# Slot masks stored by the sort and read back in the attention sums, edge masks scaled on ScalarE, and smaller first score batches

## The chip, the core and the metric

The kernel runs on one core of a Trainium2 chip. The metric is the device time of one execution in microseconds (us). A core has five engines that work side by side, each through its own queue in order: TensorE (PE, with its weight loads listed as PEld), VectorE (DVE), ScalarE (ACT), GpSimd (POOL) and SyncE (SP), which issues most DMA transfers. Engines wait for each other by semaphores.

## What is computed

A graph with 6250 nodes and 100000 edges, sorted by target node `dst`, and 128 features. Two graph layers, each followed by a residual and a layer norm:

```python
# layer 0, twice: h = x @ W
norm = dinv[src] * ew * dinv[dst]
out = segment_sum(h[src] * norm[:, None], dst) + b
# layer 1
z = h @ fc_w.T;  rh = r_h @ fc_r_w.T           # r_h: one row per edge
e = z[src] @ aw[0] + z[dst] @ aw[1] + rh @ aw[2]
e = where(e >= 0, e, 0.01 * e)
ex = exp(e - segment_max(e, dst)[dst])
alpha = ex / segment_sum(ex, dst)[dst]
agg = segment_sum(alpha[:, None] * (z[src] + rh), dst)
out = relu(agg + z @ loop_w)
```

## The kernel before, in words

**Chunks and slots.** The edges are cut into NC = 49 chunks of CC = 2048 (16 to a partition). In each chunk `sort` gives every edge a slot: a partition 0 to 127 (`pm`) and one of G = 17 groups (`pg`), so that an edge lies on one of the 32 slots that its source node's block of 128 nodes has in a group (the overflow goes to the last five groups). Twelve of the groups are served from a table of node rows in SBUF (`hot`), by matmuls with a 0/1 mask (line 475); the other five, `far`, by indirect DMA (line 484). `sort` works in batches of seven chunks. Its second half (lines 749 to 764) makes for each chunk two masks on VectorE, `ohm` (128 x 2048 bf16: which partition) and `ohg` (128 x 272 bf16: which group), multiplies `ohg` with the edge's record into `put`, and moves the records to their slots with 16 matmuls (line 763). `pm` and `pg` of all chunks stay in SBUF.

**Stages.** Preparation and degrees (to about 150 us), the first node table, then three passes over the 49 chunks:
- First convolution, 245 to 730 us. The sort's steps are dealt out between its chunks. `slot_rows` (line 833) reads each chunk's row of source numbers, spread to all partitions; `slot_masks` compares it (line 837) and stores the mask for later (line 838). Both transfers, and the sort's own store (line 773), go through SP's queue.
- Second table, and second convolution, 790 to 1224 us, in an order written out by hand. It reads the masks back (line 975), and also multiplies the edge features with a row (line 964).
- Attention. `scores` is a generator of steps: `ends` and `starts` gather the two node terms of each edge (`starts` takes a chunk in two halves: line 1071 makes a mask of a row `rk` read from DRAM, 48 matmuls of line 1078, then `sel` and `asr` on VectorE, lines 1081 and 1082); `softmax` (line 1086) works on one batch of chunks as a chain of scans, small matmuls and transfers. `batches` (line 69) sets the batch sizes: 2, 5, then 7. The sums of a batch can begin when its softmax is done.
- Sums (line 1238 on), one chunk after the other, with the next batch's score steps dealt between. `shares` (line 1180) makes `ohm` and `ohg` again from `pm` and `pg`, multiplies `ohg` with the attention shares `al3`, and moves them to the slots: `swt`, the scale of the gathered rows. `pick` gathers the rows and scales them (ScalarE, line 480), `weigh` scales five narrow masks (ScalarE, line 514), `scatter` adds rows into a window of 144 target nodes (TensorE, line 521), one chunk late. `edge_part` (line 1195) does the edge features: `ms` (128 x 16 x 32) says which of 32 targets an edge belongs to, and is multiplied by the share (line 1211, VectorE); 32 matmuls (line 1222) take it with the features `et`; ScalarE copies the result (line 1227); four more matmuls place it.

**Order.** Except in the second convolution, the order on each engine comes from a planner at build time. It takes the instructions by their place in the program, and lets a later one go first where an earlier one, by its own estimate, can't start yet. Buffers are rings: a tile with `bufs=1` is written again only when its readers are done.

Of the kernel before, what the change touches and what calls it, by code (L numbers as in the profile page):

```python
# [10 lines left out]
BF16 = mybir.dt.bfloat16  # L11
I32 = mybir.dt.int32
AF = mybir.ActivationFunctionType
OP = mybir.AluOpType
# [5 lines left out]
P = 128  # L20
# [5 lines left out]
TC = 16  # L26
CC = P * TC
NL = CC // P
WC = 144
WS = 32  # L30
# [8 lines left out]
def gnn_kernel(ctx, tc, x, src, dst, ea, ew, W1, b1, W2, b2, fcw, fcrw, attn, loopw, out):  # L39
# [11 lines left out]
    nc = tc.nc  # L51
# [14 lines left out]
    NC = CF + 1  # L66
    assert 9 <= NC <= 64

    batches, c0 = [], 0
    while c0 < NC:  # L70
        n = min((2, 5)[len(batches)] if len(batches) < 2 else 7, NC - c0)
        batches.append((c0, n))
        c0 += n
    NT = len(batches)
# [3 lines left out]
    G = GP + GS  # L78
# [17 lines left out]
    dram = ctx.enter_context(tc.tile_pool(name="dram", bufs=1, space=DRAM))  # L96
    keep = ctx.enter_context(tc.tile_pool(name="keep", bufs=1))
# [5 lines left out]
    asd_d = dram.tile([NB * P, 2], F32, name="asd_d")  # L103
    md = dram.tile([NB * P, 1], F32, name="md")
    masks = dram.tile([NC, P, GP * P], BF16, name="masks")

    adgd = dram.tile([(NC * NL + 2) * P], F32, name="adgd")
    shd = dram.tile([NC * CC], F32, name="shd")
# [16 lines left out]
    iotab = const.tile([P, WJ], BF16, name="iotab")  # L125
# [11 lines left out]
    iota_t = const.tile([P, P, TC], BF16, name="iota_t")  # L137
# [47 lines left out]
    sdst = keep.tile([P, NC, G], BF16, name="sdst")  # L185
    swt = keep.tile([P, NC, G], F32, name="swt")
    sidx = keep.tile([P, NC, GS], I32, name="sidx")

    pm = keep.tile([P, NC, TC], BF16, name="pm")
    pg = keep.tile([P, NC, TC], BF16, name="pg")  # L190

    dlb = keep.tile([P, NC, TC], BF16, name="dlb")
    rels = keep.tile([P, NC, NL], BF16, name="rels")
# [233 lines left out]
    def out_of(sum_x, sum_r, b0, n, xp, pool, tag):  # L427

        some = blocks[b0 : b0 + n]
        fin = xp.tile([P, 4, D], F32, name="fin", bufs=1)  # L430
        load_some(nc.sync, fin, x1d, b0, n)
        yield
        agg = pool.tile([P, 4, D], F32, name="agg", tag=tag)
        for b, nb in some:
            of = slice(b * P, b * P + nb)
            nc.tensor.matmul(agg[:nb, b - b0, :], sum_r[:, of], wfrT, start=True, stop=False)
            nc.tensor.matmul(agg[:nb, b - b0, :], sum_x[:, of], ident, start=False, stop=True)
        for p, k in whole(some, b0):
            nc.vector.scalar_tensor_tensor(fin[:p, k, :], agg[:p, k, :], 0.0, fin[:p, k, :], op0=OP.max, op1=OP.add)
        yield  # L440
        yield from normed(fin, some, b0, xp)
        store_blocks(nc.sync, out, fin, b0, n)
# [93 lines left out]
    grp = ed.tile([P, NC, TC], BF16, name="grp")  # L536
# [132 lines left out]
    BATCH = 7  # L669
    spilled = keep.tile([P, NC], F32, name="spilled")  # L670
    sorting = ctx.enter_context(ExitStack())
    sp = sorting.enter_context(tc.tile_pool(name="sort", bufs=2))
# [3 lines left out]
    nc.vector.memset(go_on, 1.0)  # L676
    nc.vector.memset(go_on[:, :, 0:1], 0.0)

    def sort():

        for c0 in range(0, NC, BATCH):
# [4 lines left out]
            for c in cs:  # L686
# [24 lines left out]
                k = BP  # L711
# [29 lines left out]

            nc.vector.tensor_tensor(t_, m_i[:, :n, :], r_, op=OP.subtract)
            nc.vector.tensor_mul(t_, t_, o)
            nc.vector.tensor_add(pm[:, some, :], r_, t_)
            nc.vector.scalar_tensor_tensor(t_, k_i[:, :n, :], float(GP), grp[:, some, :], op0=OP.add, op1=OP.subtract)
            nc.vector.tensor_mul(t_, t_, o)
            nc.vector.tensor_add(pg[:, some, :], grp[:, some, :], t_)
            slots = sp.tile([P, BATCH, NF], F32, name="slots")
            for c in cs:
                ohm = sp.tile([P, P, TC], BF16, name="ohm")  # L750
                nc.vector.tensor_tensor(ohm, iota_t, pm[:, c, None, :].to_broadcast([P, P, TC]), op=OP.is_equal)  # L751
                ohg = sp.tile([P, TC, G], BF16, name="ohg")
                nc.vector.tensor_tensor(ohg, iotab[:, None, :G].to_broadcast([P, TC, G]),
                                        pg[:, c, :, None].to_broadcast([P, TC, G]), op=OP.is_equal)
                put = sp.tile([P, TC, NF], BF16, name="put")
                nc.vector.tensor_tensor(put[:, :, : G * F].rearrange("p t (g f) -> p t g f", f=F),  # L756
                                        ohg[:, :, :, None].to_broadcast([P, TC, G, F]),
                                        rec[:, c, :, None, :].to_broadcast([P, TC, G, F]), op=OP.mult)
                nc.vector.tensor_tensor(put[:, :, G * F :], ohg[:, :, GP:],  # L759
                                        blk[:, c, :, None].to_broadcast([P, TC, GS]), op=OP.mult)  # L760
                ps = ps_c.tile([P, NF], F32, name="rec")
                for t in range(TC):
                    nc.tensor.matmul(ps, ohm[:, :, t], put[:, t, :], start=t == 0, stop=t == TC - 1)  # L763
                nc.scalar.copy(slots[:, c - c0, :], ps)
                yield
# [247 lines left out]
    with tc.tile_pool(name="look", bufs=2) as lp, tc.tile_pool(name="conv3", bufs=2) as wp, \  # L1013
# [162 lines left out]
        def deal(count):  # L1176
            for _ in range(count):
                next(steps, None)

        def shares(c, al3, i):  # L1180

            ohm = mp.tile([P, P, TC], BF16, name="ohm", bufs=1)
            nc.vector.tensor_tensor(ohm, iota_t, pm[:, c, None, :].to_broadcast([P, P, TC]), op=OP.is_equal)
            ohg = mp.tile([P, TC, G], BF16, name="ohg", bufs=1)
            nc.vector.tensor_tensor(ohg, iotab[:, None, :G].to_broadcast([P, TC, G]),
                                    pg[:, c, :, None].to_broadcast([P, TC, G]), op=OP.is_equal)
            put = mp.tile([P, TC, G, 3], BF16, name="put", bufs=1)
            nc.vector.tensor_tensor(put, ohg[:, :, :, None].to_broadcast([P, TC, G, 3]),
                                    al3[:, i, :, None, :].to_broadcast([P, TC, G, 3]), op=OP.mult)
            ps = ps_c.tile([P, G, 3], F32, name="rec")  # L1190
            for t in range(TC):
                nc.tensor.matmul(ps, ohm[:, :, t], put[:, t], start=t == 0, stop=t == TC - 1)  # L1192
            nc.vector.tensor_reduce(swt[:, c, :], ps, AX.X, OP.add)

        def edge_part(c, aw, i):

            k = min(NL, -(-(E - c * CC) // P))
            full = k if c < CF else crem // P
            ets = []
            for s0 in range(0, k, NL // 2):  # L1200
                et = mp.tile([P, NL // 2, D], F32, name="et", bufs=3)
                e0, m = c * CC + s0 * P, min(max(full - s0, 0), NL // 2)
                if m:
                    nc.sync.dma_start(et[:, :m, :], ea[e0 : e0 + m * P, :].rearrange("(s p) f -> p s f", p=P))
                if s0 <= full < min(k, s0 + NL // 2):
                    nc.sync.dma_start(et[: crem % P, m, :], ea[e0 + m * P : E, :])
                ets.append(et)
            ms = mp.tile([P, NL, WS], F32, name="ms", bufs=1)
            nc.vector.tensor_tensor(ms, iota[:, None, :WS].to_broadcast([P, NL, WS]),
                                    rels[:, c, :, None].to_broadcast([P, NL, WS]), op=OP.is_equal)  # L1210
            nc.vector.tensor_mul(ms, ms, aw[:, i, :, None].to_broadcast([P, NL, WS]))
            pl = mp.tile([P, NL // 8, WC], F32, name="pl", bufs=1)
            nc.vector.tensor_tensor(pl, iota[:, None, :WC].to_broadcast([P, NL // 8, WC]),
                                    place[:, :, c : c + 1].to_broadcast([P, NL // 8, WC]), op=OP.is_equal)
            ps = ps_r.tile([P, NL // 8, D], F32, name="r")
            for g in range(NL // 8):
                for half in range(2):
                    for q in range(4):
                        s = 8 * g + 2 * q + half
                        if s < k:  # L1220
                            p = P if s < full else crem % P
                            nc.tensor.matmul(ps[WS * q : WS * q + WS, g, :], ms[:p, s, :], ets[g][:p, s % 8, :], start=half == 0,
                                             stop=half == 1 or s + 1 == k)
            sw = mp.tile([P, NL // 8, D], F32, name="sw")
            ng, rest = divmod((k + 1) // 2, 4)
            if ng:
                nc.scalar.copy(sw[:, :ng, :], ps[:, :ng, :])
            if rest:
                nc.scalar.copy(sw[: WS * rest, ng, :], ps[: WS * rest, ng, :])
            ps = ps_c.tile([P, WC], F32, name="rec")  # L1230
            sizes = [P] * ng + ([WS * rest] if rest else [])
            for g, p in enumerate(sizes):
                nc.tensor.matmul(ps, sw[:p, g, :], pl[:p, g, :], start=g == 0, stop=g == len(sizes) - 1)
            return ps

        pieces = Pieces(lambda b0, n: out_of(acc2, sum_r, b0, n, xp, ps_c, "rec"))
        held = None
        for b, (c0, n) in enumerate(batches):
            while b not in ready:
# [212 lines left out]
```

## Time and profile before

| What | us |
|---|---|
| Median of 3 runs (2057.70, 2063.59, 2058.34) | 2058.34 |
| The profiled execution | 2054.54 |
| Its span | 2052.7 |
| Busy in the span: TensorE / VectorE | 1612.4 / 1641.2 |
| Busy in the span: ScalarE / GpSimd | 940.8 / 1097.1 |

The page of the profile shows one execution. Its groups of instructions have the form "line, engine, operation, out<-in, shape, count | busy us, mean ns of one | idle time of the engine just before", and its views of waits name who waited for whom. Over the whole span TensorE and VectorE look alike (79% and 80% busy), so the stages have to be looked at one by one. The mean granted TensorE clock is 0.885. The core moves 306.80 MB by DMA in the span, 149 GB/s.

### The profile page before, as it was taken

The page shows a single profiled execution, that of the slowest core. Times are in us where ns is not written, and L with a number is a line of the kernel's source. Part 1 is how long each engine was busy: PE and PEld are TensorE (multiplying, and loading weights), DVE is VectorE, ACT ScalarE, POOL GpSimd, SP SyncE. Part 2 cuts the span into 40 slices and gives each one's busy share as a digit, 9 for nine tenths or more (in the row PEclk, how much of TensorE's full clock was granted, in tenths as well). Part 3 has the DMA queues.
Part 4 walks back from the last instruction along what each step waited for, and adds up shares of the span by engine and source line. Part 5 has one row for each costly group of instructions (what it writes and reads, how often), then busy time and mean ns, then how long its engine had stood idle before and what let it go on. Part 6 is the DMA issues. An engine that isn't in the chain of part 4 may idle for free.

```text
span 2052.7 us, 78879 instructions
## 1 busy us (share of the span) xinstructions
PE 1612.4 (79%) x33861; PEld 1460.6 (71%) x33861; DVE 1641.2 (80%) x3271; ACT 940.8 (46%) x3096; POOL 1097.1 (53%) x954
## 2 busy tenths in 40 slices
PE   2668689889798886788898885367888888989985
PEld 2456478778788765687787874257777777888885
DVE  8665988779788535899899894589989998998673
ACT  1104355454454655466676773113343434445543
POOL 5001666676675635888788881312434343535662
PEclk9767699899899977899999996568999999999998
DMA  3001343343442625687777775945656666665662
GB/s 70 24 1 37 94 127 112 101 129 95 117 115 70 209 56 193 177 246 222 239 243 244 246 235 156 134 128 139 185 163 192 171 198 171 177 178 158 182 178 67
DMA packets 260707, 306.80 MB, mean 149 GB/s; under 512 B 44121, under 2 KB 199372, under 8 KB 253299
## 3 DMA queue, kind: packets, MB, share of 16 engines
q1 hardware_dynamic: 228741, 244.80, 38.8%
q0 software_dynamic: 23520, 48.22, 11.4%
q10 hardware_dynamic: 8088, 8.65, 1.4%
q8 instruction: 268, 4.39, 0.9%
q14 instruction: 90, 0.74, 0.1%
HBM read 260.35 MB, written 41.23 MB: 147 GB/s over the span
## 4 chain that ended last, share of the span: by engine, by line
DVE 37%; PE 36%; DMA 12%; issue 8%; ACT 5%; POOL 2%; SPq 1%; DVEq 1%; POOLq 0%; ACTq 0%
PE win L521 15%; DVE wm L490 6%; PE g L475 6%; DVE sel L1081 3%; DVE put L756 2%; DMA et<-in_edge_attr_dram 2%; DMA rk<-srow 2%; DMA far<-g,sidx 2%; DMA mask<-srd 2%; DVE et L964 2%; PE rec L1192 2%; ACT got L480 2%; PE mm L332 2%; DVE ohm L751 1%; PE r L706 1%
## 5 line engine op out<-in xcount | busy, mean ns | idle before, releaser
L484 POOL DMA_INDIRECT far<-g,sidx x490 | 707.1, 1443 | 238.6 <-PE win L521 112.0
L480 ACT ACTIVATE got<-g,swt 128x128 f32<-128x128 f32 x1764 | 487.4, 380 | 350.6 <-PE g L475 152.4
L484 POOL DMA_INDIRECT far<-zd,sidx x245 | 311.4, 1271 | 449.9 <-PE win L521 329.1
L521 PE MATMUL win<-wm,got 128*128 128x144 f32 x3528 | 522.0, 306 | 12.4 <-issue 12.2
L521 PEld LDWEIGHTS win<-wm,got 128*128 128x128 f32 x3528 | 485.6, 204 | 30.6 <-issue 21.0
L475 PE MATMUL g<-hot,mask 128*32 128x128 bf16 x21168 | 384.2, 226 | 90.8 <-issue 68.4
L475 PEld LDWEIGHTS <-mask 128*32 128x32 bf16 x21168 | 327.1, 100 | 124.5 <-issue 99.9
L490 DVE TENSOR_TENSOR wm<-iota,sdst 128x1728 f32<-128x1728 f32 x147 | 286.7, 1950 | 4.4 <-DMA g<-rows 4.4
L514 ACT ACTIVATE wm<-wm,swt 128x64 f32<-128x64 f32 (+1 forms) x735 | 203.1, 357 | 99.6 <-DVE wm L497 63.4
L521 PE MATMUL win<-wm,far 128*128 128x64 f32 (+1 forms) x1470 | 186.9, 273 | 11.6 <-DMA far<-g,sidx 11.2
L521 PEld LDWEIGHTS win<-wm,far 128*128 128x128 f32 x1470 | 182.4, 195 | 12.7 <-issue 12.7
L321 POOL TENSOR_TENSOR hot<-low,hot 128x512 bf16<-128x512 f32 x24 | 42.2, 1759 | 199.7 <-DVE own L714 130.4
L1078 PE MATMUL k<-adp,rk 128*128 128x49 bf16 x2352 | 91.4, 194 | 66.3 <-DVE sel L1081 52.0
L1078 PEld LDWEIGHTS <-rk 128*128 128x128 bf16 x2352 | 83.7, 103 | 77.9 <-DVE rk L1071 42.6
L964 DVE TENSOR_TENSOR et<-et,ar_row 128x2048 f32<-128x2048 f32 (+1 forms) x49 | 111.6, 2278 | 23.7 <-DMA et<-in_edge_attr_dram 23.7
L526 DVE TENSOR_TENSOR acc<-acc,win 128x144 f32 x147 | 44.4, 302 | 96.8 <-PE win L521 85.7
L965 DVE TENSOR_REDUCE dots<-et 128x16 f32<-128x2048 f32 (+1 forms) x49 | 112.0, 2286 | 1.7
L763 PE MATMUL rec<-put,ohm 128*128 128x90 bf16 x784 | 62.0, 254 | 34.5 <-DVE put L759 33.6
L763 PEld LDWEIGHTS <-ohm 128*128 128x128 bf16 x784 | 56.9, 165 | 41.4 <-DVE put L759 33.7
L1081 DVE TENSOR_TENSOR sel<-k,ohb 128x392 f32<-128x392 f32 x98 | 83.6, 853 | 2.5 <-PE k L1078 2.1
L756 DVE TENSOR_TENSOR put<-ohg,rec 128x1360 bf16<-128x1360 bf16 x49 | 76.8, 1567 | 0.0
L709 ACT CAST own<-r 128x768 bf16<-128x768 f32 x49 | 39.7, 810 | 75.0 <-PE r L706 49.3
(390 smaller groups left out, 2375.7 us busy)
## 6 DMA issues: line engine op xcount, KB each, us to landing
et<-in_edge_attr_dram SPq DMA_DIRECT2D x97, 512.0 KB
et<-in_edge_attr_dram SPq DMA_DIRECT2D x48, 1024.0 KB
mask<-masks SPq DMA_DIRECT2D x98, 384.0 KB
rk<-srow SPq DMA_DIRECT2D x98, 256.0 KB
mask<-srd SPq DMA_DIRECT2D x49, 384.0 KB
masks<-mask SPq DMA_DIRECT2D x49, 384.0 KB
far<-g,sidx POOLq DMA_INDIRECT x490
g<-rows SPq DMA_DIRECT2D x24, 256.0 KB
```

What stands on the lines that cost most here:

```text
L475: nc.tensor.matmul(ps[32 * q : 32 * q + 32, g, :], mask[:, (g0 + g) * P + 32 * q : (g0 + g) * P + 32 * q + 32], hot[:, 4 * (g0 + g) + q, k ...
L480: nc.scalar.activation(got[:, g, :], ps[:, g, :], AF.Copy, scale=swt[:, c, g0 + g : g0 + g + 1])
L484: nc.gpsimd.indirect_dma_start(out=got, out_offset=None, in_=table[:, :], in_offset=bass.IndirectOffsetOnAxis(ap=sidx[:, c, g : g + 1], ax ...
L490: nc.vector.tensor_tensor(wm[:, : GP * WC].rearrange("p (g w) -> p g w", w=WC), iota[:, None, 1 : WC + 1].to_broadcast([P, GP, WC]), sdst[ ...
L514: nc.scalar.activation(m, m, AF.Copy, scale=swt[:, c, g : g + 1])
L521: nc.tensor.matmul(ps[:, n0 : n0 + m.shape[-1]], rows[g], m, start=g == 0, stop=g == G - 1)
L756: nc.vector.tensor_tensor(put[:, :, : G * F].rearrange("p t (g f) -> p t g f", f=F), ohg[:, :, :, None].to_broadcast([P, TC, G, F]), rec[: ...
L763: nc.tensor.matmul(ps, ohm[:, :, t], put[:, t, :], start=t == 0, stop=t == TC - 1)
L964: nc.vector.tensor_mul(et[:n], et[:n], ar_row[:n, None, :].to_broadcast([n, TC, D]))
L965: nc.vector.tensor_reduce(dots[:n, c, :], et[:n], AX.X, OP.add)
L1078: nc.tensor.matmul(ps[:, s, :], mk[:, s * P : (s + 1) * P], adp[:, 0, k, :NB], start=k == 0, stop=k == 2)
L1081: nc.vector.tensor_mul(sel, ps, ohb.rearrange("p b s -> p s b"))
```

## The change

Three edits go together. The sort now keeps each chunk's two masks in one tile `slot` (128 x 2320 bf16: `ohm` and `ohg` side by side) and stores it to a DRAM tensor `slotd`; `pm` and `pg` become temporaries. The sums read `slotd` back, one chunk ahead, with two buffers. In `edge_part` the product of `ms` and the share becomes up to sixteen activations on ScalarE, one for each run of 128 edges, with the share as the scale. And the batches become 2, 3, 4, 5, then 7 chunks: nine batches instead of eight.

```diff
-        n = min((2, 5)[len(batches)] if len(batches) < 2 else 7, NC - c0)
+        n = min((2, 3, 4, 5)[len(batches)] if len(batches) < 4 else 7, NC - c0)
...
+    slotd = dram.tile([NC, P, P * TC + TC * G], BF16, name="slotd")
...
-    pm = keep.tile([P, NC, TC], BF16, name="pm")
-    pg = keep.tile([P, NC, TC], BF16, name="pg")
...
+    def slot_views(slot):
+        return (slot[:, : P * TC].rearrange("p (q t) -> p q t", t=TC),
+                slot[:, P * TC :].rearrange("p (t g) -> p t g", g=G))
...
-            nc.vector.tensor_add(pm[:, some, :], r_, t_)
+            pm = sp.tile([P, BATCH, TC], BF16, name="pm")
+            pg = sp.tile([P, BATCH, TC], BF16, name="pg")
+            nc.vector.tensor_add(pm[:, :n, :], r_, t_)
...
-                ohm = sp.tile([P, P, TC], BF16, name="ohm")
-                nc.vector.tensor_tensor(ohm, iota_t, pm[:, c, None, :].to_broadcast([P, P, TC]), op=OP.is_equal)
-                ohg = sp.tile([P, TC, G], BF16, name="ohg")
+                slot = sp.tile([P, P * TC + TC * G], BF16, name="slot")
+                ohm, ohg = slot_views(slot)
+                nc.vector.tensor_tensor(ohm, iota_t, pm[:, c - c0, None, :].to_broadcast([P, P, TC]), op=OP.is_equal)
                 nc.vector.tensor_tensor(ohg, iotab[:, None, :G].to_broadcast([P, TC, G]),
-                                        pg[:, c, :, None].to_broadcast([P, TC, G]), op=OP.is_equal)
+                                        pg[:, c - c0, :, None].to_broadcast([P, TC, G]), op=OP.is_equal)
+                nc.sync.dma_start(slotd[c], slot)
...
+        slots_in = {}
+
+        def load_slots(c):
+            if c < NC:
+                slots_in[c] = mp.tile([P, P * TC + TC * G], BF16, name="slot", bufs=2)
+                nc.sync.dma_start(slots_in[c], slotd[c])
+
         def shares(c, al3, i):
-            ohm = mp.tile([P, P, TC], BF16, name="ohm", bufs=1)
-            nc.vector.tensor_tensor(ohm, iota_t, pm[:, c, None, :].to_broadcast([P, P, TC]), op=OP.is_equal)
-            ohg = mp.tile([P, TC, G], BF16, name="ohg", bufs=1)
-            nc.vector.tensor_tensor(ohg, iotab[:, None, :G].to_broadcast([P, TC, G]),
-                                    pg[:, c, :, None].to_broadcast([P, TC, G]), op=OP.is_equal)
+            ohm, ohg = slot_views(slots_in.pop(c))
+            load_slots(c + 1)
...
-            nc.vector.tensor_mul(ms, ms, aw[:, i, :, None].to_broadcast([P, NL, WS]))
+            for s in range(k):
+                nc.scalar.activation(ms[:, s, :], ms[:, s, :], AF.Copy, scale=aw[:, i, s : s + 1])
...
         pieces = Pieces(lambda b0, n: out_of(acc2, sum_r, b0, n, xp, ps_c, "rec"))
+        load_slots(0)
```

More of the change, by code (lines that the diff above doesn't have):

```diff
@@ L743, in sort @@
             nc.vector.tensor_mul(t_, t_, o)
-            nc.vector.tensor_add(pm[:, some, :], r_, t_)
+            pm = sp.tile([P, BATCH, TC], BF16, name="pm")
+            pg = sp.tile([P, BATCH, TC], BF16, name="pg")
+            nc.vector.tensor_add(pm[:, :n, :], r_, t_)
             nc.vector.scalar_tensor_tensor(t_, k_i[:, :n, :], float(GP), grp[:, some, :], op0=OP.add, op1=OP.subtract)
             nc.vector.tensor_mul(t_, t_, o)
-            nc.vector.tensor_add(pg[:, some, :], grp[:, some, :], t_)
+            nc.vector.tensor_add(pg[:, :n, :], grp[:, some, :], t_)
             slots = sp.tile([P, BATCH, NF], F32, name="slots")
             for c in cs:
-                ohm = sp.tile([P, P, TC], BF16, name="ohm")
-                nc.vector.tensor_tensor(ohm, iota_t, pm[:, c, None, :].to_broadcast([P, P, TC]), op=OP.is_equal)
-                ohg = sp.tile([P, TC, G], BF16, name="ohg")
+                slot = sp.tile([P, P * TC + TC * G], BF16, name="slot")
+                ohm, ohg = slot_views(slot)
+                nc.vector.tensor_tensor(ohm, iota_t, pm[:, c - c0, None, :].to_broadcast([P, P, TC]), op=OP.is_equal)
                 nc.vector.tensor_tensor(ohg, iotab[:, None, :G].to_broadcast([P, TC, G]),
-                                        pg[:, c, :, None].to_broadcast([P, TC, G]), op=OP.is_equal)
+                                        pg[:, c - c0, :, None].to_broadcast([P, TC, G]), op=OP.is_equal)
+                nc.sync.dma_start(slotd[c], slot)
                 put = sp.tile([P, TC, NF], BF16, name="put")
```

## The prediction

> **What bounds the kernel now.** I read first the busy times by stretch, with the borders set at the stages (first convolution 245 to 730 us, second 790 to 1224, sums from 1357, the point 1881 where the scores are done). Columns: busy of PE, PEld, DVE, ACT, POOL, granted clock, DMA share, GB/s.
>
> ```profile
> 245.00:730.00 485.00, 421.84 (x9609) 390.68 (x9602) 382.91 (x785) 260.68 (x910) 331.55 (x240) 0.93 0.41 120
> 790.00:1224.00 434.00, 361.02 (x8670) 333.85 (x8674) 394.32 (x422) 285.68 (x937) 356.18 (x235) 0.94 0.75 235
> 1290.00:1357.00 67.00, 25.91 (x495) 22.85 (x497) 46.20 (x117) 4.55 (x13) 15.90 (x12) 0.52 0.86 138
> 1357.00:1406.00 49.00, 31.15 (x647) 27.87 (x639) 42.04 (x131) 10.06 (x38) 6.29 (x5) 0.69 0.51 134
> 1406.00:1881.00 475.00, 407.77 (x9599) 375.55 (x9598) 444.76 (x1055) 188.80 (x646) 203.42 (x165) 0.97 0.63 174
> 1881.00:2033.00 152.00, 138.23 (x3214) 132.22 (x3213) 102.57 (x197) 78.27 (x283) 91.26 (x64) 0.99 0.60 162
> ```
>
> From 1406 to 1881, 33 chunks of the sums run beside the scores: VectorE is 94% busy and TensorE 86%, at 14.4 us a chunk. In the last 14 chunks no scores are left: VectorE falls to 67%, TensorE rises to 91%, 10.9 us a chunk. So the sums are VectorE's first and TensorE's later. The first convolution leaves VectorE a fifth of its time and the DMA engines more than half.
>
> Second, who waits for whom from 1406 to 1881 (us in total, times, longest):
>
> ```profile
> ACT got L480 <- DVE swt L1193: 125.5, 29, 8.5
> ...
> PE rec L1192 <- DVE put L1188: 15.6, 17, 1.6
> PE k L1078 <- DVE sel L1081: 15.4, 17, 3.3
> ...
> DVE rk L1071 <- DMA rk<-srow: 5.6, 4, 3.6
> ```
>
> Both other engines wait for VectorE. ScalarE idles 125.5 us for shares that VectorE delivers late; VectorE itself hardly waits for a transfer.
>
> Third, what the edit touches, as the groups of that stretch and the one line of ohg have it:
>
> ```profile
> L1183 DVE TENSOR_TENSOR ohm<-iota_t,pm 128x2048 bf16<-128x2048 bf16 x33 | 40.1, 1215 | 0.0
> ...
> L1211 DVE TENSOR_TENSOR ms<-ms,aw 128x512 f32<-128x512 f32 x32 | 21.6, 675 | 0.0
> ```
> ```profile
> L1185 DVE TENSOR_TENSOR ohg<-iotab,pg x49: 407/433/472, 1293.4 to 1999.8; 128x272 bf16<-128x272 bf16 x49
> ```
>
> None of the three is preceded by idle time: they are queued back to back, so their removal shortens the queue.
>
> **What the Trainium skill says.** "ScalarE: Activation LUTs", What ACT_TABLE_LOAD costs: an activation takes 186 ns plus 0.833 ns an element, some 93 ns more for each pointer operand, and neighbours overlap by some 93 ns. For 32 columns with a pointer scale an estimate of 306 ns, 213 ns start to start. The trace agrees for the next sizes (ScalarE's timeline, five of 64 columns, then eight of 128):
>
> ```profile
> 1579.50 1.30 ACT L514 ACTIVATE wm<-wm,swt 128x64 f32<-128x64 f32 x5 [1.88 <-DVE wm L497]
> 1582.31 2.18 ACT L480 ACTIVATE got<-g,swt 128x128 f32<-128x128 f32 x8 [1.50 <-PE win L521]
> ```
>
> With one at 0.36 and 0.38 us, (1.30 - 0.36) / 4 is 0.24 us a step at 64 columns, (2.18 - 0.38) / 7 is 0.26 at 128. "TensorE: Matmul & The Clock Gate", Architectural detail, says that ScalarE and VectorE are strictly first in, first out: a waiting instruction holds all behind it. The 125.5 us above are such a wait. "DMA: Bandwidth & Descriptors", Queues, rings and completion order: transfers issued by one sequencer share one ring on each DMA engine, taken in order. So a new store can delay a read issued after it; the trace of before has no such pair to show it.
>
> **The change, part by part.** Each number is against the profiled execution: 2054.5 us for a span of 2052.7; the median of the runs shown is 2058.3, so 3.8 us are added at the end.
>
> *Masks read back.* Per chunk of the sums VectorE loses ohm 1.215 and ohg 0.433. *Edge masks on ScalarE* takes the product ms, 0.68. Together 2.33 us a chunk, for the 35 chunks before 1881: 82 us. *More batches*: nine softmax passes for eight. One costs VectorE 8.6 us (the groups of lines 1102 to 1144 and the splits of al, over six passes, 51.7 us), and ScalarE two table loads of 1.28. The number of end and start steps is the same, their place is not: before chunk 2 can start, three chunks' scores are needed and not five. That is four halves fewer ahead of it, each sel 0.86, asr 0.56, rk 0.48 and ohb 0.35 on VectorE, 9 us; they come back later. The wider row tables (nine rows for eight) add under 1 us in the second convolution, beside its transfers.
>
> So for 1357 to 1881 VectorE has 42.0 + 444.8 - 82 + 8.6 = 413 us of work, TensorE 31.2 + 407.8 + 1.5 for the extra pass = 440. TensorE becomes the longer. How near to 100% it gets is my choice: I take 91%, what it shows in the last 14 chunks where VectorE no longer holds it. 440 / 0.91 = 484 against 524: **-40 us**. Bounds: at the 86% of now 513, -11; at 95%, 463, -61.
>
> *ScalarE's new link.* Sixteen activations at 0.21 to 0.24 us, 3.4 to 3.8 us a chunk (782 in all). From 1406 to 1881 ScalarE is 40% busy and has the room. In the last 14 chunks 5.6 us of 10.9 become 9.1, 84%. There the product lies between the mask on VectorE and TensorE's 32 r matmuls, with 12 got and 5 wm activations in the same queue. The r matmuls start 5 to 9 us after VectorE's product today (1944.0 to 1949.0, 1952.9 to 1960.1), so 3.5 us fit unless the got block goes first. Behind a late r on TensorE stand the rec, next share and next g matmuls. VectorE's saving there is worth nothing. **+4 us**; bounds -2 and +20 (1.4 us a chunk).
>
> *Sort's stores.* 49 of 128 x 2320 bf16, 594 KB each. At the second convolution's rate (235 GB/s at 0.75 share, 313 GB/s full) one holds the engines 1.9 us. VectorE's next use of a slot buffer now waits for its store, two chunks back; behind it stands all of VectorE's work, and TensorE waits for that. On SP the store waits for ohg; behind it stand the masks' stores, the srd store and the srd reads. Those reads already come late in the first convolution (engines' waits there):
>
> ```profile
> DVE mask L837 <- DMA mask<-srd: 29.5, 15, 3.0
> ```
>
> If all 15 grow by 1.9 us, 28 us; if the stores fit between, nothing. Below nothing I exclude, as no work leaves the stage. I take a third: **+9 us**.
>
> *Slot reads.* 49 of 594 KB on SP, a chunk ahead, two buffers. DMA work per chunk of the sums: 0.63 x 14.4 = 9.1 us, plus 1.9 is 11.0 in some 13.3: 83%, more than the 75% of the second convolution. I cost that inside the 91%. Ahead of the sums it is different: between 1290 and 1357 the DMA share is 0.86 and the first rk reads stand on the chain of waits:
>
> ```profile
> 1305.62 11.21 DMA rk<-srow
> ...
> 1322.21 5.79 DMA rk<-srow
> ```
>
> Two slots at that stretch's 138 GB/s are 8.6 us if put ahead of rk, 0 behind: **+4 us**.
>
> Sum: -40 + 4 + 9 + 4 = -23. 2054.5 - 23 = 2031.5 profiled, **2035** as a median.
>
> **The rivals.**
> *TensorE fully fed.* The scores' matmuls (line 1078) fill its gaps, since VectorE then has 15% to spare: 463 us, -61, with +3 elsewhere: 2000. For it: every large wait of TensorE names VectorE. Against it: at 83% DMA share reads arrive later.
> *The gain goes into transfers.* The rk reads run only two halves ahead; at a higher DMA share VectorE's 5.6 us of waits grow, TensorE stays at 86%: -11, +4 in the tail, +5 and +2: 2058, no change.
> *The first convolution pays* and the kernel ends slower. Every chunk there needs one mask read in time, and each now shares its ring with a 1.9 us store; in the worst case 49 x 1.9 = 93 us. The rest of the sum is -32, so from 0.65 us a chunk this decides. At 1.1 us, 54 - 32 = +22: 2080. For it: 15 reads are late already, and SP's queue is in order. Against it: 34 are not late, and the DMA share is 0.41.
>
> **How the numbers follow.** My forecast 0.55 (2018 to 2050), TensorE fully fed 0.18, gain lost to transfers 0.13, first convolution pays 0.14. A measurement here tells about 0.3%, 6 us. Faster: 0.55 + 0.18 + a sixth of 0.13 is 0.75; slower 0.14; the rest, 0.11, within. The range leaves out half of the best case below and most of the slow one above: 2000 to 2066.
>
> **What would show it.** Right: ohm and ohg gone from VectorE in the sums, sixteen activations of 128x32 a chunk at 0.21 to 0.24 us a step, 35 chunks from 1357 in some 484 us with TensorE near 91%, the wait of got for swt well below 125 us, the first convolution within 10 us of 485. Wrong: PE r waiting for ACT ms often in the last 14 chunks; DVE rk waiting for its read by tens of us; DVE mask or sort's ohm waiting for transfers for over 60 us.

## The result: 0.4% slower, and the profile after

| | before | after |
|---|---|---|
| Median of 12 runs each | 2058.4 | 2067.1 |
| Ratio after / before, 95% interval | | 1.0038 (1.0013 to 1.0063) |
| The profiled execution / its span | 2054.5 / 2052.7 | 2058.8 / 2057.0 |
| Busy: TensorE / VectorE | 1612 / 1641 | 1629 / 1558 |
| Busy: ScalarE / GpSimd | 941 / 1097 | 1105 / 1094 |
| Moved by DMA | 306.8 MB | 365.1 MB |

VectorE lost 83 us of covered time (time in which at least one of its instructions runs) and the kernel became 0.4% longer. The forecast was 2035.

The stretches of after, with the columns of the prediction's first view (busy of PE, PEld, DVE, ACT, POOL, granted clock, DMA share, GB/s); the borders are the same events as before:

```profile
245.00:722.00 477.00, 416.19 (x9574) 386.98 (x9573) 379.65 (x782) 261.28 (x914) 328.97 (x237) 0.94 0.53 165
1353.00:1393.00 40.00, 26.51 (x579) 23.27 (x577) 31.04 (x94) 13.09 (x54) 6.18 (x5) 0.73 0.48 131
1393.00:1882.00 489.00, 421.93 (x9588) 383.25 (x9587) 400.05 (x1010) 302.48 (x1171) 203.71 (x163) 0.97 0.73 213
1882.00:2037.00 155.00, 140.72 (x3270) 131.90 (x3269) 75.13 (x156) 119.03 (x492) 86.51 (x67) 1.00 0.71 209
```

Read the third line against the 475 us of before. VectorE is busy 82% of it instead of 94%, ScalarE 62% instead of 40%, the DMA share is 0.73 instead of 0.63. TensorE stands at 86%, where it stood. It was expected at 91%.

The waits of after from 1393 to 1882 (us in total, times, longest):

```profile
ACT ms L1222 <- DVE ms L1219: 38.2, 18, 3.8
...
DVE acc L525 <- PE win L520: 31.1, 18, 5.2
...
ACT got L479 <- DVE swt L1203: 24.2, 16, 6.5
...
PE k L1084 <- DVE sel L1087: 22.2, 26, 3.4
DVE rk L1077 <- DMA rk<-srow: 21.3, 23, 2.9
...
PE rec L1244 <- ACT sw L1238: 7.0, 16, 1.4
...
PE r L1233 <- ACT ms L1222: 1.4, 3, 0.6
```

Two lines of the same view of before, from 1406 to 1881:

```profile
DVE acc L526 <- PE win L521: 7.2, 14, 1.2
...
PE rec L1233 <- ACT sw L1227: 4.2, 10, 1.0
```

The wait of got for the shares fell from 125.5 to 24.2 us, and the 15.6 us in which TensorE waited for put are gone (0.7 us are left). That is what the edit was to do. But VectorE now waits itself: for the windows of scatter 31.1 us (7.2 before), for the row reads 21.3 (5.6). TensorE's own waits in this view, all rows added, are 65 us; in the same view of before they are 66. What put gave back stands under sel (15.4 to 22.2), sw (4.2 to 7.0) and "issue", idle time for which the profile names no one waited for (about 1 to 7).

From chunk 14 on the batches are alike in both kernels. Here are chunks 14 to 35, first before, then after, then e8 below, a run of the change with the old batches:

```profile
1576.00:1881.00 305.00, 263.78 (x6149) 242.50 (x6148) 284.96 (x673) 122.03 (x414) 132.13 (x106) 0.96 0.63 174
```
```profile
1580.00:1882.00 302.00, 256.91 (x5877) 236.95 (x5876) 232.96 (x571) 194.66 (x748) 128.04 (x103) 0.95 0.71 210
```
```profile
1573.00:1892.00 319.00, 266.30 (x6118) 246.32 (x6117) 246.47 (x603) 196.65 (x755) 131.39 (x107) 0.94 0.70 208
```

The same chunks don't hold the same score work, since the steps of the scores run ahead of the sums, and further ahead after the smaller batches. `sel` runs once for each half of a chunk's scores; its own busy time and count in these stretches, in the same order:

```profile
1576.00:1881.00 305.00, 39.62 (x46) 0.96 0.63 174
```
```profile
1580.00:1882.00 302.00, 34.43 (x40) 0.95 0.71 210
```
```profile
1573.00:1892.00 319.00, 39.72 (x46) 0.94 0.70 208
```

In after VectorE is covered for 52 us less and the 21 chunks take 3 us less, but with six halves less in them (some 13 us of VectorE's time). With the same 46 halves, e8 takes 14 us more than before. So VectorE's saving turned into idle time of VectorE, and at equal work the stretch became longer. e8 ran on another chip of the same kind; the three traces of the whole change (after, e5, e17) differ by 3 us in this stretch, 299.7 to 302.5. Over chunks 0 to 35 the score work is nearly equal: 82 halves before, 81 in after and in e8.

Where the profiled execution gained and lost, by the same events in both traces (a second trace of the same changed kernel, e17 below, beside it; differences to before in us):

| Stretch | predicted | after | e17 |
|---|---|---|---|
| start to the last edge features of the second convolution (1255.6 before) | +9 | -11.9 | -4.8 |
| from there to the first shares of the sums (103.7) | +4 | +7.8 | +6.5 |
| chunks 0 to 35 of the sums (522.1) | -40 | +5.1 | +8.4 |
| last 14 chunks and the end (171.3) | +4 | +3.3 | +2.8 |
| sum | -23 | +4.3 | +12.9 |

### The profile page after: what moved, and what is told of

Same layout as the page of the kernel before. It is cut to its first block, busy times and chain, and to the rows that moved or that the text cites. A ratio compares the mean times of both kernels' runs of the same rounds, so it can differ in the third digit from the quotient of the medians.

```text
span 2057.0 us, 79778 instructions
## 1 busy us (share of the span) xinstructions
PE 1629.1 (79%) x33871; PEld 1466.1 (71%) x33871; DVE 1558.4 (76%) x3150; ACT 1104.9 (54%) x3880; POOL 1093.9 (53%) x954
## 4 chain that ended last, share of the span: by engine, by line
PE 31%; DVE 21%; DMA 11%; ACT 7%; issue 6%; POOL 1%; SPq 1%; DVEq 0%; POOLq 0%; ACTq 0%
PE win L520 14%; PE g L474 5%; DMA rk<-srow 4%; DVE wm L489 4%; ACT got L479 2%; DVE et L970 2%; DVE sel L1087 2%; DMA et<-in_edge_attr_dram 2%; ACT ms L1222 2%; PE k L1084 2%; PE r L1233 2%; PE rec L1202 2%; PE mm L331 1%; DMA far<-g,sidx 1%; PE rec L1244 1%
## 5 line engine op out<-in xcount | busy, mean ns | idle before, releaser
L483 POOL DMA_INDIRECT far<-zd,sidx x245 | 307.2, 1254 | 469.4 <-PE win L520 352.5
L474 PE MATMUL g<-hot,mask 128*32 128x128 bf16 x21168 | 395.3, 226 | 82.3 <-issue 63.7
L474 PEld LDWEIGHTS <-mask 128*32 128x32 bf16 x21168 | 334.2, 100 | 115.4 <-issue 95.1
L1222 ACT ACTIVATE ms<-ms,aw 128x32 f32<-128x32 f32 x782 | 176.7, 318 | 50.3 <-DVE ms L1219 46.9
L320 POOL TENSOR_TENSOR hot<-low,hot 128x512 bf16<-128x512 f32 x24 | 38.1, 1590 | 196.3 <-DVE own L717 129.6
L769 PE MATMUL rec<-put,slot 128*128 128x90 bf16 x784 | 61.6, 252 | 35.5 <-DVE put L765 34.7
L769 PEld LDWEIGHTS <-slot 128*128 128x128 bf16 x784 | 56.5, 165 | 42.4 <-DVE put L765 34.9
L1233 PE MATMUL r<-et,ms 128*32 128x128 f32 x1564 | 80.0, 282 | 4.1 <-ACT ms L1222 4.0
```

The source lines that it names most:

```text
L474: nc.tensor.matmul(ps[32 * q : 32 * q + 32, g, :], mask[:, (g0 + g) * P + 32 * q : (g0 + g) * P + 32 * q + 32], hot[:, 4 * (g0 + g) + q, k ...
L483: nc.gpsimd.indirect_dma_start(out=got, out_offset=None, in_=table[:, :], in_offset=bass.IndirectOffsetOnAxis(ap=sidx[:, c, g : g + 1], ax ...
L1222: nc.scalar.activation(ms[:, s, :], ms[:, s, :], AF.Copy, scale=aw[:, i, s : s + 1])
```

## The experiments

Three theories of why VectorE's saving brought nothing were put to test. **A:** the row reads `rk` of the scores come late because the slot reads share their queue and engines, and they set the pace. **B:** ScalarE's sixteen activations set the pace of TensorE's r matmuls, which run while the activations run. **C:** the smaller batches cost more than they bring.

Kernels of one group ran on one chip, each against the kernel before on that chip. Two of the groups fell on chips where the kernel before takes 2058 to 2061 us, three on chips where it takes 2386 to 2442; ratios are compared within each kind.

### Where the kernel before takes 2386 us: each part alone

**e1: the slots alone.** The changes of `slotd`, `slot` and `load_slots` are kept; batches and the product of `ms` are as before.

> Only the slot masks are stored and read back; the product of ms stays on VectorE and the batches stay 2, 5, 7. Theory A (the rk reads of the scores are the new limit: their waits on VectorE grew from 5.6 to 21 us in the stretch of the scores, and their share of the chain there from 4% to 14%): the 1.65 us a chunk that VectorE saves is mostly given back, 2045 to 2062 us, and the waits of VectorE's line for rk grow to 15 us or more. Theory B (ScalarE's sixteen activations pace TensorE's r matmuls, whose busy time grew from 36 to 53 us): the slots alone are a gain, 2020 to 2040 us. Theory C (smaller batches cost): also 2020 to 2040 us.

Measured: 2366.9 against 2386.5, ratio 0.9945 (0.9908 to 0.9982).

**e2: the activations alone.**

```diff
-            nc.vector.tensor_mul(ms, ms, aw[:, i, :, None].to_broadcast([P, NL, WS]))
+            for s in range(k):
+                nc.scalar.activation(ms[:, s, :], ms[:, s, :], AF.Copy, scale=aw[:, i, s : s + 1])
```

> Only the product of ms goes to ScalarE. Theory A: a small gain or nothing, 2045 to 2058 us, since no transfer is added. Theory B: slower, 2062 to 2080 us, with the r matmuls busy 25 us longer in the sums. Theory C: a gain, 2030 to 2050 us.

Measured: 2357.4, ratio 0.9901 (0.9858 to 0.9944).

**e3: the batches alone.**

```diff
-        n = min((2, 5)[len(batches)] if len(batches) < 2 else 7, NC - c0)
+        n = min((2, 3, 4, 5)[len(batches)] if len(batches) < 4 else 7, NC - c0)
```

> Only the batches are 2, 3, 4, 5, 7. Theories A and B: within 8 us of before (one more softmax pass, a start some 9 us earlier). Theory C: slower by 8 us or more.

Measured: 2391.8, ratio 1.0026 (1.0002 to 1.0050).

**e4: the whole change, rows read three halves ahead.** Four small constants were moved to pools that end early, to make room for the fourth buffer (in e6 and e7 below too).

```diff
-                rks[i] = lp.tile([P, HC], BF16, name="rk", bufs=3)
+                rks[i] = lp.tile([P, HC], BF16, name="rk", bufs=4)
...
-                sources(2 * c + h + 2)
+                sources(2 * c + h + 3)
```

> The whole change, with the rk reads issued three halves ahead into four buffers, not two into three (four small constants are moved to pools that end early, to make room). Theory A: VectorE's waits for rk fall back below 8 us and the time falls by 15 us or more against the change, to 2050 or less. Theory B: no change against the change as it stands, 2060 to 2070 us. Theory C: the same, 2060 to 2070 us.

Measured: 2364.4, ratio 0.9912 (0.9881 to 0.9944).

This chip is not the one of the result. All four kernels, and before, are some 16% longer here, and about half of the added time sits where none of the edits is. TensorE's idle time under "issue" ahead of the gathers g, over the whole span, first the profile of before above, then e2:

```profile
PE g L475 <- issue: 68.4, 37, 6.0
```
```profile
PE g L475 <- issue: 228.3, 481, 6.1
```

68 us in 37 pieces became 228 us in 481, 160 of the 295 us by which e2's profile is longer; it is 212 us in e4, 224 in e3 and 227 in e1. So TensorE has gaps here that none of the edits is aimed at, and the parts' values can't be carried over to the chip of the result. The questions were asked again there.

### Where the kernel before takes 2061 us: theories B and C, and the price of a read

**e5: the changed kernel again**, as the base of this group.

> The whole change as it stands, once more, beside the next three on one chip: the yardstick for them, and for the single parts, which ran where the kernel before took 2386 us. If the parts add up there (slots -0.6%, activations -1.0%, batches +0.3%), it is 1.3% faster than before; if the parts hinder each other, or if the chip decides, it is not.

Measured: 2067.2 against 2061.2, ratio 1.0040 (1.0021 to 1.0059): the result repeats.

**e6: a second buffer for ms**, so that a chunk's mask and activations can run while TensorE still reads the last one's.

```diff
-            ms = mp.tile([P, NL, WS], F32, name="ms", bufs=1)
+            ms = mp.tile([P, NL, WS], F32, name="ms", bufs=2)
```

> The whole change with two ms buffers instead of one (four small constants are moved to pools that end early, to make room), so that the sixteen activations can run a chunk ahead of TensorE's r matmuls. If the activations pace TensorE (theory B): r matmuls busy 15 us less or more in the sums, and 10 us or more faster than the change as it stands. If the rk reads are the limit (theory A): within 6 us of it.

Measured: 2073.7, ratio 1.0081 (1.0055 to 1.0107). Slower still.

**e7: the kernel before with an added read of 549 KB a chunk** that nobody uses, from SP's queue; the rest is computed as before.

```diff
+                extra = mp.tile([P, 1072], F32, name="extra", bufs=1)
+                e0 = min(c + 1, CF - 1) * CC
+                nc.sync.dma_start(extra, ea[e0 : e0 + CC, :].rearrange("(p t) f -> p (t f)", t=TC)[:, :1072])
```

> The kernel before with one more read of 549 KB a chunk in the sums, of edge features into a tile that nobody uses (the same four constants are moved for room): the transfer of the slots without the work that it saves. If added transfers delay the reads of rk (theory A): slower than before by 10 us or more, with VectorE's waits for rk above 15 us between 1400 and 1880. Otherwise within 6 us of before.

Measured: 2081.4, ratio 1.0105 (1.0080 to 1.0129). As nobody reads the buffer, nothing held the reads to their chunks: all 49 were issued between 1320 and 1635 us, each holding SP's queue for the one before (88.1 us in 30 waits):

```profile
SPq L1259 <- DMA extra<-in_edge_attr_dram: 88.1, 30, 7.3
```

Chunk 0 came 12 us later, chunks 0 to 14 of the sums took 239 us instead of 217, and the later ones were unchanged. VectorE's waits for rk in chunks 0 to 35 were 13.3 us, for 5.6. That shows the price of a train of reads in this queue, not of one read a chunk.

**e8: slots and activations with the old batches** (2, 5, 7).

> Slots and activations, with the batches left at 2, 5, 7. If the smaller batches cost (theory C), 6 us or more faster than the whole change; otherwise within 6 us of it.

Measured: 2072.2, ratio 1.0075 (1.0049 to 1.0101). So on this chip the new batches do not cost: without them the kernel is about 0.35% slower than with them, though the two intervals overlap. In the profiles chunks 0 to 35 take 538 us in e8 and 527 to 531 in the three of the whole change (after, e5, e17). Theory C falls here. And the loss is in the other two edits: with the batches, the softmax passes (seven) and nearly the halves (81 for 82) of before, e8 takes 538 us for these chunks where before takes 522.

e8 and e6 also speak to B. TensorE's group of r matmuls in the stretch from 1393 to 1882 (covered us, mean ns of one, idle just before), of after, e8 and e6:

```profile
L1233 PE MATMUL r<-et,ms 128*32 128x128 f32 x1050 | 53.2, 277 | 1.5 <-ACT ms L1222 1.4
```
```profile
L1233 PE MATMUL r<-et,ms 128*32 128x128 f32 x1009 | 38.3, 277 | 0.0
```
```profile
L1235 PE MATMUL r<-et,ms 128*32 128x128 f32 x1018 | 41.7, 280 | 0.0
```

Before, this group took 38.1 us. In after the r matmuls are stretched only in chunks 2 to 14 (28.3 us, for 12.3 before); from chunk 14 on they run at full speed (24.9 us, for 23.9), and there too the saving brings nothing. In e6 they take 20.0 us in chunks 2 to 14, 8 less than in after, and these chunks take 194 us, for 187. In e8 they run at nearly full speed and show no wait for an activation in this stretch, yet its chunks 2 to 35, which hold the scores of two chunks and one softmax less than after, take 491.8 us against 489.3 in after and 475.0 before. In e6 these chunks take 495.8. Were B the cause, both would have won back the 11 to 15 us by which r is shorter. So B falls, as far as it speaks of r. ScalarE reaches TensorE a second way, by the copy sw of r's result: TensorE's wait for it is 14.6 us in e8's chunks 2 to 35, for 4.2 before and 7.0 in after. In chunks 14 to 35 of e8 none of ScalarE's time between the end of r and that copy went to activations of ms; got, wm and the layer norm of the output stood there.

### Where the kernel before takes 2387 and 2442 us: pairs of parts

**e9 and e13: activations and batches, masks made in the sums as before.** The two are one kernel on two chips.

> The whole change without the slots: activations and batches only, no added transfer. Theory A (added reads make the rk reads late): the waits of VectorE's line for rk between 1400 and 1880 fall to 10 us or less, and it is 10 us or more faster than the whole change, 2040 to 2055 us where that takes 2067. Theory B (the activations hold TensorE): no faster than the whole change, 2062 us or more.

> The whole change without the slots, to be read on a chip where the kernel before takes some 2060 us. Theory A: 2040 to 2055 us, waits for rk at most 10 us. Theory B: 2062 us or more.

Measured: 0.9980 (0.9943 to 1.0016) and 0.9953 (0.9923 to 0.9983).

**e10 and e14: slots and batches, the product of ms on VectorE as before.**

> The whole change without the activations: slots and batches, the product of ms on VectorE. Theory A: like the whole change, 2060 to 2072 us, since the added reads are still there. Theory B: faster than before, 2035 to 2052 us, with the r matmuls busy 15 us less than in the whole change.

> The whole change without the activations, to be read on a chip where the kernel before takes some 2060 us. Theory A: 2060 to 2072 us, waits for rk as in the whole change. Theory B: 2035 to 2052 us, r matmuls busy 15 us less in the stretch from 1393 to 1882.

Measured: 0.9953 (0.9925 to 0.9981) and 0.9988 (0.9959 to 1.0016). VectorE's waits for rk in chunks 0 to 35 are 11.0 and 15.4 us here, 4.0 and 1.9 in e9 and e13. So the slot reads do make the rows late, as A says; but e9 is not faster than e10, and the intervals of e13 and e14 overlap.

**e11 and e15: e4's kernel again.**

> The whole change with the rk reads three halves ahead, once more: its first run met a chip on which the kernel before took 2386 us, and the whole change was not run there. Theory A: 10 us or more faster than the whole change, 2057 us or less where that takes 2067, with VectorE's waits for rk halved. If the lateness of the rk reads follows the stage and doesn't set it: within 6 us of the whole change.

> The whole change with the rk reads three halves ahead, to be read on a chip where the kernel before takes some 2060 us. Theory A: 2057 us or less. If the lateness of the rk reads doesn't set the stage: 2061 to 2073 us.

Measured: 0.9969 (0.9933 to 1.0005) and 0.9958 (0.9922 to 0.9994).

**e12: the whole change with the slot reads in GpSimd's queue**, so that no row read stands behind one.

```diff
-                nc.sync.dma_start(slots_in[c], slotd[c])
+                nc.gpsimd.dma_start(slots_in[c], slotd[c])
```

> The whole change with the slots read from GpSimd's queue and not from SP's, so that the rk reads no longer stand behind a 580 KB read in SP's rings. If it is the place in the rings that makes the rk reads late: their waits halve and it is 10 us or more faster than the whole change. If it is the load on the DMA engines as such, or the distance of the reads: within 6 us of it.

Measured: 1.0018 (0.9982 to 1.0055). Not better than e11 beside it, which keeps the slots in SP's queue and reads the rows earlier. VectorE's waits for rk in chunks 0 to 35 are 15.5 us, not half of the 11.0 in e10, which reads the slots from SP's queue.

**e16: e2's kernel again**, beside e13.

> Only the product of ms on ScalarE, to be read on a chip where the kernel before takes some 2060 us. Theory A: 2045 to 2058 us. Theory B: 2062 to 2080 us.

Measured: 2392.1 against 2441.8, ratio 0.9788 (0.9729 to 0.9847).

On these chips the activations alone are the best version, by 1.0 and 2.1% (eight and six runs). With the batches added (e13) 0.5% is left of e16's 2.1%: here the smaller batches cost, against what e8 shows on the other kind of chip. With the slots added as well (e11 beside e9, e15 beside e13) nothing is added. And the whole change with deeper row reads (the change itself did not run on these chips) is 0.3 to 0.9% faster here, while below it is 0.6% slower. So the sign of this version belongs to the chip; that of the change itself may.

### Where the kernel before takes 2059 us: theory A

**e17: the changed kernel a third time. e18: with rows read three halves ahead**, e4's kernel.

> The whole change as it stands, beside the next run on one chip. Where the kernel before takes 2060 us: 0.4% slower than before, as twice already. Where it takes 2380 us or more: unknown until now; the runs with one part left out lie between 0.2% and 0.5% below before there, so the whole change should too.

> The whole change with the rk reads three halves ahead, paired with the run before this one. Theory A (late rk reads set the stage): 0.5% or more faster than the whole change, on either kind of chip. If their lateness only follows from the pace of the other engines: within 0.3% of it.

Measured: 1.0044 (1.0025 to 1.0062) and 1.0057 (1.0034 to 1.0079). The row wait and the stretch, first of e17, then of e18:

```profile
DVE rk L1077 <- DMA rk<-srow: 25.1, 25, 2.8
```
```profile
1393.00:1882.00 489.00, 422.66 (x9603) 383.85 (x9606) 400.18 (x1024) 300.02 (x1172) 201.22 (x160) 0.96 0.73 211
```
```profile
DVE rk L1079 <- DMA rk<-srow: 17.1, 14, 2.4
```
```profile
1393.00:1882.00 489.00, 419.14 (x9552) 383.28 (x9541) 395.25 (x1002) 299.97 (x1167) 195.92 (x161) 0.95 0.73 210
```

A had a good case on paper. In the chain of waits of this stretch the row reads hold 4.0% before, 14.0% in after and 16.1% in e17. The median time from issue to use fell from 8.8 us before to 6.0 in after; half of the reads had less than 6 us. The deeper reads did what they were for: 7.1 us, 26 reads under 6 us instead of 49, 8 us less waiting, 10.7% of the chain. Chunks 2 to 35 took 490.3 us, against 490.9 in e17. The waits went elsewhere (acc for win 28.1 to 33.6 us, TensorE's total from 65 in after to 68). So a third less of this wait is worth nothing: A falls as the cause of the pace, at least for the part of the wait that was removed.

## Why the prediction was wrong, step by step

**The work removed: right, its cover not.** The summed durations of VectorE's groups for chunks 0 to 35 fell from 573.8 to 501.2 us, 73 us, the very sum of the prediction (82 - 8.6). But the covered time fell from 487 to 431 us, 56, where the prediction went from 487 to 413. The records of instructions that stand back to back overlap (573.8 summed, 487 covered), so part of each removed duration lay under its neighbour. A saving on a full queue has to be cut by that ratio: 0.85 x 73 is 62.

**TensorE rises to 91%: this step failed**, and with it the -40 us. The prediction took the busy share of the last 14 chunks as the share that TensorE reaches "where VectorE no longer holds it". VectorE stopped holding the shares, as said, and TensorE went from 439 of 524 us (84%) to 448 of 529 (85%). Its bounds, -11 to -61, took for granted that TensorE keeps at least its 86% on a smaller sum of work plus 1.5 us; its covered time grew by 9.5, as the stretched r matmuls alone took 15 more (53 us for 38 from chunk 2 on). Chunks 0 to 35 became 5 to 8 us longer in place of 40 shorter; with slots and activations alone (e8) they became 16 us longer. The two stages differ in more than VectorE's load: with scores in the queue TensorE has the k matmuls that wait for sel, and the small matmuls of the softmax that wait for scans, and these waits were 37 us before (sel, rk, part, full and e in the waits from 1406 to 1881) and are 40 in after. So the shorter queue of VectorE left these waits as they were. Why is argued below, not shown.

**The early start: the size came out, the reason only in part.** The stretch from chunk 0 to chunk 2 fell from 47 to 38 us (9 were forecast, for four halves fewer). But `sel` ran 24 times ahead of chunk 2's shares before and 22 times in after: two halves fewer, 4.5 us of VectorE's time. The masks of two chunks, 4.7 us, left VectorE in the same stretch. So the agreement is in part luck. Chunks 2 to 14 then took 187 us for 170. They hold 36 halves for 28, some 18 us of VectorE's time, and one softmax more, 8.6 us, against 28 us of masks less. Beside e8 the new batches are worth 7 to 11 us in chunks 0 to 35, so what is missing is the gain of the slots and activations, not that of the batches.

**ScalarE's link: right.** Fourteen activations of a chunk, in ScalarE's timeline of after:

```profile
1683.17 3.08 ACT L1222 ACTIVATE ms<-ms,aw 128x32 f32<-128x32 f32 x14
```

Their group on the page of after:

```profile
L1222 ACT ACTIVATE ms<-ms,aw 128x32 f32<-128x32 f32 x782 | 176.7, 318 | 50.3 <-DVE ms L1219 46.9
```

With one at 0.318 us, (3.08 - 0.32) / 13 is 0.21 us a step. The estimate from the Trainium skill ("ScalarE: Activation LUTs", What ACT_TABLE_LOAD costs) was 306 and 213 ns, and the trace agrees at this size. At 128 columns, where the prediction also called it in agreement, the same estimate gives 0.29 us a step, and its trace line shows 0.26 (got, read from PSUM). The last 14 chunks and the end became 3 us longer, 4 were forecast. TensorE waited there for the activations 1.8 us in all; acc waits for win 61.7 us: VectorE is ahead there, busy for 75 of 155 us.

**Sort's stores: wrong in sign.** Forecast +9. VectorE's waits for a slot buffer whose store is under way are 0.7 us, in two places, and the mask wait stands at 30.7 us against 29.5:

```profile
DVE mask L843 <- DMA mask<-srd: 30.7, 17, 5.0
...
DVE slot L757 <- DMA slotd<-slot: 0.7, 2, 0.5
```

The stores fit between. The first convolution is 8 us shorter, the second ends 5 to 12 us earlier; why it is shorter and not equal was not tested.

**Slot reads ahead of the sums: right in kind, too small.** +8 and +6 for +4; the first rows wait 23.6 us for 18.3 before, 5 of the 8.

**The rivals.** "The gain goes into transfers" names a time, 2058, near the measured one, and TensorE's 86%, but not the cause. The sign that the prediction named for it did come, VectorE waiting for rk by tens of us (21 and 25), but e18 removed a third of that wait without effect. "The first convolution pays" ended on the measured side for a reason that the trace excludes.

**What stays open.** The size of a chunk from 14 to 35 (14.5 us before, 14.4 in after with six halves less, 15.2 in e8 at equal work) is not explained by any one engine, transfer or link that was tried. Argued, not shown: the engines' queues are in order (the Trainium skill, "TensorE: Matmul & The Clock Gate", Architectural detail, says so of ScalarE and VectorE; no run here tests it), the scores' matmuls have one PSUM buffer, so k of the next half waits for sel, sel for k, and the rest of each queue stands behind. In favour: in after TensorE waits 22.2 us for sel, VectorE 31.1 us for win, each for the other. A second PSUM buffer for k, which would test it, was not tried.

A rival that no run tests is the order itself. The planner orders each kernel anew, by its own estimates, so an edit moves more than its own instructions. In chunks 14 to 35 of before, the win matmuls stand on TensorE in 51 pieces, 12 times with k matmuls alone between two of them. In e8, with the same halves, they stand in 28 pieces, and never so. How much of the 14 us by which e8 is longer there comes from this order, and how much from transfers or from ScalarE, isn't known; a run with the order of before and the work of after would show it.

Also open is the value of each single part on a chip of the result's kind: e1, e2 and e3 fell on another, and so did both runs of the best version there, the activations alone.

## What to carry to other kernels

When an engine is 94% busy and the others wait for it, taking work off it moves the end only if the next engine has work ready in those moments (here 82 us came off and the stretch grew); look for waits in both directions between the two (here k for sel, acc for win) before pricing the gain at the next engine's rate. Don't take the busy share of a stage without some of the work as what the stage with that work will reach. Before two stretches are called alike, count an instruction in both (here sel, 46 and 40). And cut a saving by the overlap of the records: summed against covered time of the engine in that stretch.

## What the hardware showed beside this

- The same single-core programs take 16 to 19% longer on some chips: the kernel before has medians of 2386, 2387 and 2442 us on two of them, 2058 to 2061 on the others. There TensorE idles under "issue" ahead of the 128x32 mask matmuls in 463 to 531 places of up to 6.4 us, 211 to 262 us in all, for 68 in 37 places before; the granted clock of the profiled runs is 0.83 to 0.85, for 0.885.
- An edit can have opposite signs on the two kinds of chip: with deeper row reads the whole change has 0.9912 to 0.9969 on the one, 1.0057 on the other.
- Reads into a buffer that no instruction uses don't keep to the loop that they stand in: they went out as a train, and each held SP's queue for up to 7.3 us.
